# A graph network's edge stage and tile periods: new lags and beats, large accumulators for keys, values and down projections, sums transposed behind the gate

## The chip, the core and the metric

The kernel runs on one core of a Trainium2 chip. The metric is the device time of one execution in microseconds (us), the median of the runs. One execution was also recorded by the hardware profiler, and every duration below is of that one. The engines are TensorE (PE: matrix products; PEld is its weight load), VectorE (DVE), ScalarE (ACT), GpSimd (POOL) and SyncE (SP). SP, ACT and POOL also issue DMAs, each in the order of its own instructions.

## What is computed

Two layers of a graph network run over 625 nodes with 1024 features and 10000 edges, followed by a mixture of experts. The change lies in the first layer. Cut to it, the reference is:

```python
xn = _layernorm(x)
x = x + graph_attention(xn, edges) + linear_attention(xn)   # both read the same xn
x = x + ffn(_layernorm(x))          # gate, up and down, weights cut to -1, 0, 1
xn = _layernorm(x)                  # from here the second layer
...
def graph_attention(x, src, dst):
    x = rmsnorm(x) @ W_down
    xl, xr = x @ Wl, x @ Wr
    e = sum_over_64(leaky_relu(xl[src] + xr[dst]) * att)    # four heads for every edge
    alpha = softmax of e over the edges of one dst
    return segment_sum(alpha * xl[src], dst) @ W_up
```

## The kernel before

Nodes are taken in five tiles of 125 (t = 0 to 4), features in eight chunks of 128. Products are in float32, and one product of the source is two MATMUL instructions in the profile. The order of every engine's instructions is written out by hand (a manual schedule). A small queue `do` spreads a step over time: `do(prep, pe, after, after2)` writes the PE work now, `after` at the next call of `do`, and `after2` at the one behind that. So the place of a call in the code sets its place on each engine.

**Edge stage** (about 50 to 430 us). PE works on the linear attention: keys and values of all tiles (`key`, `value`) in two halves c = 0 and 1, counts of edges (`count`), queries and answers, then its output projection in pieces (`mixed`). Beside it, POOL, DVE and ACT work on the edges in *beats* of two columns of 128 edges. In a beat, POOL gathers rows of xl and xr (`gather`, lines 585 to 593), DVE adds and weighs those of an earlier beat (`score_group`), ACT takes the exponential (`raise_all`), and POOL scatters an older result into a table in DRAM (`scatter`). `lags = [3, 4, 5]` says how many beats behind the gather the score, the exponential and the scatter are. Four buffers hold gathered rows. PE's program calls `work(us)` behind each piece of its work, and a beat is written out when the sum of these passes a due time:

```python
while beat["us"] >= 8.0 + 5.2 * min(beat["g"], 5) + 8.1 * max(beat["g"] - 5, 0) and chunks:
```

Beats 1 to 5 also hold the self loops of one tile each. From the end of the queries on, the lags are 1, 1 and 2. `weight_sums` (line 741, DVE) and `weight_means` (a small product pm on PE) make the scales of the feed-forward weights, and `ternary` cuts them.

**The gate.** When the last scatter is in the table, `load_table(t)` fetches the exponentials of all edges into tile t, in `[src, dst]` order: two DMAs, 1.2 MB. `weigh(t)` on DVE multiplies them by the edge counts, and `sums(t)` on PE (pg) adds them up. Table 0 goes through ACT's queue, tables 1 to 4 and the five tiles of x (0.5 MB each) through POOL's.

**Tile periods** (p = 0 to 6, about 430 to 620 us). In period p, tile p gets its sums (pg), the division go, the transpose `turn_sums` (pgoT, copied by ACT to goT) and the product with W_up (`up_again`, px). Tile p - 1 gets the feed-forward network: statistics and quantisation on DVE (p1), transposes (f1, ptr), gate and up products (f2, pgu), a transpose (f3, phT), and the down product (f4, pdn). Tile p - 2 is normalised and transposed for the second layer (p5, f5). From period 2 on, keys and values of the second layer (pk, pv; `spacer`) fill in. Their weights are 4 MB, issued by SP (`lin1.weights(0)`).

PSUM has two pools of accumulators there: `ps1`, two of 512 columns, and `ps2`, three of twice 512. A new accumulator waits until an old one of its kind has been read. The output projection holds three large ones until `up_again` of tiles 0, 1 and 2 has added to them.

`class LinearAttention` (line 216) serves both layers: `half(c)` loads weights and two rows of biases, broadcast to 128 partitions.

Of the kernel before, what the change touches and what calls it, by code (L numbers as in the profile page):

```python
# [8 lines left out]
FP = mybir.dt.float32  # L9
# [44 lines left out]
def attempt(ctx: ExitStack, tc: tile.TileContext, w: dict, out: bass.AP, shifted: bool):  # L54
# [161 lines left out]
    class LinearAttention:  # L216


        def __init__(self, xnT, names, bq, work, rows_on):
            self.xnT, self.names, self.work, self.rows_on = xnT, names, work, rows_on  # L220
            self.bq = mix.tile([128, KC], FP, tag="bq", name="bq", bufs=2)
            rows_on.dma_start(out=self.bq, in_=bq)
            self.kv = []
# [8 lines left out]

        def half(self, c, loaded=False):
            Wk, bk, Wv, bv = (w[n] for n in self.names[1:])
            if not loaded:
                self.weights(c)
            self.bk, self.bv = self.bias(bk, c, "bk_t"), self.bias(bv, c, "bv_t")
            self.kf = mid([P, NT, 512], "kf")
            self.v = mid([P, NT, 4, 129], "v")
            nc.gpsimd.memset(self.v[:, :, :, 128:129], 1.0)  # L240
            self.kv.append(mix.tile([128, 4, 256], FP, tag="kv", name="kv", bufs=2))

        def key(self, t):
            kf, bk, wk = self.kf, self.bk, self.wk

            def pe():
                hold["pk", t] = ps1("pk")
                group(hold["pk", t][:P], [(self.xnT[:, k, nodes(t)], wk(k)) for k in range(KC)])

            def after():  # L250
                kb = mix.tile([P, 512], FP, tag="kb", name="kb", bufs=1)
                nc.vector.tensor_tensor(kb, hold.pop(("pk", t))[:P], bk[:P], op=ALU.add)
                ke = mix.tile([P, 512], FP, tag="ke", name="ke", bufs=1)
                nc.scalar.activation(ke, kb, AF.Exp)
                nc.scalar.activation(kb, kb, AF.Relu)
                hold["k", t] = ke, kb

            def after2():
                ke, kb = hold.pop(("k", t))
                nc.vector.scalar_tensor_tensor(kf[:, t, :], ke, 1.0, kb, op0=ALU.min, op1=ALU.add)  # L260

            do(None, pe, after, after2)
            self.work(7.0)

        def value(self, t):
            v, bv, wv = self.v, self.bv, self.wv

            def pe():
                hold["pv", t] = ps1("pv")
                group(hold["pv", t][:P], [(self.xnT[:, k, nodes(t)], wv(k)) for k in range(KC)])  # L270

            def after():
                nc.vector.tensor_tensor(v[:, t, :, 0:128],  # L273
                                        hold.pop(("pv", t))[:P].rearrange("p (a b) -> p a b", a=4),
                                        bv[:P].rearrange("p (a b) -> p a b", a=4), op=ALU.add)

            do(None, pe, after)
            self.work(7.0)
# [64 lines left out]
    with ExitStack() as st0:  # L343
# [8 lines left out]
        with ExitStack() as edges:  # L352
# [232 lines left out]
            def gather(g, j, side):  # L585
                lo, n, p = groups[g]
                if j == 0 and side == 0:
                    ab[g] = [pool.tile([128, G, 256], FP, tag=k, name=k, bufs=4) for k in ("ga", "gb")]
                if j < n:
                    src, ix = ((xl_d, si), (xr_d, di))[side]  # L590
                    nc.gpsimd.indirect_dma_start(  # L591
                        out=ab[g][side][0:p, j, :], out_offset=None, in_=src[:, :],
                        in_offset=bass.IndirectOffsetOnAxis(ap=ix[0:p, lo + j:lo + j + 1], axis=0))
# [9 lines left out]

            def scatter(last):

                if chunks and chunks[0][0] <= last:
                    g, j = chunks.pop(0)
                    lo, n, p = groups[g]
                    nc.gpsimd.indirect_dma_start(  # L609
                        out=table[:, :],  # L610
                        out_offset=bass.IndirectOffsetOnAxis(ap=at[0:p, lo + j:lo + j + 1], axis=0),
                        in_=es[0:p, lo + j, :], in_offset=None)
# [33 lines left out]


            beat = dict(us=0.0, g=0, scored=0, raised=0)
            lags = [3, 4, 5]

            def scores(last):
                while beat["scored"] <= min(last, len(groups) - 1):
# [1 line left out]
                    beat["scored"] += 1  # L654

            def raise_all(last):
                while beat["raised"] <= min(last, len(groups) - 1):
                    lo, n, p = groups[beat["raised"]]
                    exp(es[0:p, lo:lo + n, :])
                    beat["raised"] += 1  # L660

            def one_beat():
                g = beat["g"]
                beat["g"] += 1
                if 1 <= g <= NT:
                    self_loops(g - 1)
                if lags[1] > lags[0]:
                    raise_all(g - lags[1])
                    scores(g - lags[0])
                else:  # L670
                    scores(g - lags[0])
                    raise_all(g - lags[1])
                for j in range(G):
                    if g < len(groups):
                        gather(g, j, 0)
                        if lags[1] == lags[0]:
                            scatter(g - lags[2])
                        gather(g, j, 1)
                    scatter(g - lags[2])

            def work(us):
                beat["us"] += us

                while beat["us"] >= 8.0 + 5.2 * min(beat["g"], 5) + 8.1 * max(beat["g"] - 5, 0) and chunks:
                    one_beat()

            work(0.0)
# [27 lines left out]
                f()  # L715


            def mixed(t, ks=range(KC), keep=None):
                for c in range(2):
                    def pe(c=c):  # L720
                        if c == 0 and ks[0] == 0:
# [8 lines left out]
                            nc.vector.tensor_tensor(keep[:, c, :], px[:P, c, :], bo[c][:P], op=ALU.add)  # L730

                    do(None, pe, after if keep is not None and c == 1 else None)
                    work(0.87 * len(ks))

            dn = main.tile([128, 2, D], BF, name="dn")
            part3 = main.tile([128, 3], FP, name="part3")
            wmean = main.tile([128, 3], FP, name="wmean")
            wscale = main.tile([128, 3], FP, name="wscale")
# [23 lines left out]
                                        op0=ALU.subtract)  # L762

            for m in range(KC):
                if m + 1 < KC:
                    lin.query(m + 1)
                else:
                    mixed(0, range(6))
# [8 lines left out]
            wu = wpool.tile([128, 2, D], FP, tag="w", name="wu")  # L777
            nc.sync.dma_start(out=wu, in_=w["W_up"].rearrange("(k p) n -> p k n", p=128))
            bo = [lin.bias(w["L0_bo"], c, tag) for c, tag in enumerate(("bk_t", "bv_t"))]
            gu = wpool.tile([128, KC, 512], BF, tag="w", name="gu", padded_shape=[128, KC, 512])  # L780
            made = [gu[:, :, 0:256], gu[:, :, 256:512], dn]
            lags[:] = 1, 1, 2
            kept = mid([P, 2, 2, 512], "kept")
            mixed(3, keep=kept[:, 0])
            weight_sums()
            mixed(4, keep=kept[:, 1])
            weight_means()
            mixed(0, range(6, KC))
# [12 lines left out]
        late = st0.enter_context(tc.tile_pool(name="l0r", bufs=1, reuse_waits="tile"))  # L801


        def load_table(t, eng=nc.gpsimd):

            hold["tb", t] = mid([P, NT, P, 4], "tb")
            if not shifted:
                rows_dma(eng, hold["tb", t].rearrange("p s d h -> p s (d h)"),
                         tview[:, :, t * 4 * P:(t + 1) * 4 * P])

        def weigh(t):
# [105 lines left out]
        def ffn(t):  # L917
# [55 lines left out]

            def f4():
                def pe():
                    hold["pdn"] = [ps1("pdn") for c in range(2)]
                    for c in range(2):
                        group(hold["pdn"][c][:P], [(hT[:, k, 0:P], dn[:, k, c * 512:(c + 1) * 512])
                                                   for k in range(2)])

                def after():
                    rd = late.tile([P, 1], FP, tag="rd", name="rd", bufs=2)
                    nc.vector.tensor_scalar(rd, wmean[:P, 2:3], rh[:, t:t + 1], None, op0=ALU.mult)
                    for c in range(2):
                        xc = x[:, t, c * 512:(c + 1) * 512]
                        nc.vector.scalar_tensor_tensor(xc, hold["pdn"][c][:P], rd, xc, op0=ALU.mult, op1=ALU.add)  # L986

                do(None, pe, after)

# [16 lines left out]
            return p1, f1, f2, f3, f4, p5, f5  # L1006


        load_table(0, nc.scalar)
        for t in range(NT):  # L1010
            rows_dma(nc.gpsimd, x[:, t, :], xrows[t])
        load_table(1)
# [9 lines left out]
        for p in range(NT + 2):  # L1022
# [3 lines left out]
            if 1 <= p <= NT:  # L1026
                made_of[p - 1] = ffn(p - 1)
                made_of[p - 1][0]()
            if p >= 3:
                spacer()  # L1030
            if p >= 2:
                made_of[p - 2][6]()
            if p == 0:
                xnT1 = bigT("xnT1")
                nc.gpsimd.memset(xnT1[:, :, N:NP], 0.0)
                lin1 = LinearAttention(xnT1, ("L1_Wq", "L1_Wk", "L1_bk", "L1_Wv", "L1_bv"), w["L1_bq"],
                                       lambda us: None, nc.gpsimd)
            if p < NT:
                sums(p)
            if 1 <= p <= NT:  # L1040
                made_of[p - 1][1]()
                do()
                made_of[p - 1][2]()
            do()
            if p + 1 < NT:
                weigh(p + 1)
            if p + 2 < NT:
                load_table(p + 2)
            for t in ((0, 1), (2, 3, 4))[p] if p < 2 else ():
                for c in range(2):  # L1050
                    xc = x[:, t, c * 512:(c + 1) * 512]
                    nc.vector.tensor_tensor(xc, xc, bo[c][:P] if t < 3 else kept[:, t - 3, c, :], op=ALU.add)
            if p == 0:
                lin1.weights(0)
            if p == 1:
                lin1.half(0, loaded=True)
            if 2 <= p <= NT:
                spacer()
            if p < NT:
                turn_sums(p)  # L1060
            if 1 <= p <= NT:
                made_of[p - 1][3]()
            do()
# [867 lines left out]
```

## Time and profile before

| | |
|---|---|
| median of 3 runs | 2233.98 us |
| lowest, highest | 2232.08, 2243.11 us |
| the profiled execution | 2229.6 us |
| its span, first to last instruction | 2227.7 us |
| mean granted PE clock | 0.979 |
| PE busy | 2121.2 us, 95% of the span |
| POOL busy | 341.9 us, 15% |
| last scatter of the edge stage starts | 412.5 us |
| first sums of period 0 (pg) start | 433.4 us |

How to read the lines: a timeline has the start, the duration, the engine, the line of the kernel and the operation, output <- inputs with shapes, and in brackets how long the engine had been idle before and what released it. A list of waits has the engine and the tile it was about to write, what it waited for, the sum in us, the number of times and the longest. L130 is the line of a helper through which nearly all products go, so one goes by the names of tiles. A table of windows gives the busy time of each engine in a stretch, the granted clock as a part of full speed, and what the DMAs moved.

### The profile page before, as it was taken

To read this page: it belongs to the slowest core of one execution; us is meant where nothing else is said; L and a number is where in the kernel's file an instruction comes from. 1 tells how busy PE (TensorE), PEld (TensorE's weight loads), DVE (VectorE), ACT (ScalarE), POOL (GpSimd) and SP (SyncE) were. 2 spreads that over 40 slices of the span, in tenths; PEclk is the share of its full clock that TensorE was granted. 3 is DMA by queue.
4 is the path that set the end of the run, shared out by engine and by line. 5 is a ranking of instruction groups with operands and counts; after the bars stand their busy time and mean duration, and the time that the engine had idled before them with its cause. 6 is when DMAs were issued, how large, how long until landed. Compare 5 with 4: busy or idle time off the path is not lost. (4 is left out here: it accounts for less than half of the span.)

```text
span 2227.7 us, 17364 instructions
## 1 busy us (share of the span) xinstructions
PE 2121.2 (95%) x6934; PEld 1213.9 (54%) x6934; DVE 715.2 (32%) x1216; ACT 194.5 (9%) x354; POOL 341.9 (15%) x349
## 2 busy tenths in 40 slices
PE   7999898778899989999999999999999999999998
PEld 6665574444455667754445767557744444444443
DVE  4866395566521670000113133322010111111112
ACT  2100110011211110000000111110000000000000
POOL 1677777300000130010000000110000000000011
PEclk9999999869999999999999999999999999999999
DMA  9343342530122110231213111031199987997742
GB/s 289 116 136 109 119 139 86 153 92 0 38 85 76 48 48 0 76 142 38 76 38 104 38 38 38 20 103 55 41 346 337 331 325 282 327 330 287 275 144 92
DMA packets 146246, 301.62 MB, mean 135 GB/s; under 512 B 12361, under 2 KB 23052, under 8 KB 146152
## 3 DMA queue, kind: packets, MB, share of 16 engines
q1 hardware_dynamic: 123412, 243.18, 30.7%
q0 software_dynamic: 17408, 46.22, 6.8%
q10 hardware_dynamic: 5332, 10.97, 1.6%
q8 instruction: 58, 0.95, 0.2%
q14 instruction: 36, 0.29, 0.0%
HBM read 277.49 MB, written 22.84 MB: 135 GB/s over the span
## 5 line engine op out<-in xcount | busy, mean ns | idle before, releaser
L130 PE MATMUL pu<-w,xgT 128*128 128x512 f32 x768 | 333.9, 593 | 1.9 <-DVE xgT L1225 1.9
L130 PEld LDWEIGHTS pu<-w,xgT 128*128 128x128 f32 x768 | 144.0, 190 | 174.8 <-issue 171.7
L130 PE MATMUL pyb<-w,hb 128*128 128x512 f32 x384 | 174.3, 598 | 2.4 <-ACT yb L105 2.1
L130 PE MATMUL pq<-xnT,w 128*128 128x313 f32 x512 | 140.6, 434 | 9.4 <-DVE v L273 8.1
L130 PE MATMUL pv<-w,xnT 128*125 128x512 f32 x320 | 142.7, 599 | 4.7 <-DVE x L986 4.7
L130 PE MATMUL pk<-w,xnT 128*125 128x512 f32 x320 | 140.6, 592 | 0.0
L130 PE MATMUL p<-tT,w 128*128 128x313 f32 x512 | 136.3, 428 | 0.4 <-DVE tT L1225 0.4
L130 PEld LDWEIGHTS pq<-xnT,w 128*128 128x128 f32 x512 | 98.1, 193 | 50.5 <-DVE v L273 9.0
L130 PEld LDWEIGHTS pyb<-w,hb 128*128 128x128 f32 x384 | 69.8, 189 | 90.9 <-issue 74.8
L1765 DVE TENSOR_TENSOR su<-pu,su 128x512 f32<-128x512 f32 x24 | 16.6, 691 | 314.6 <-ACT su L1764 314.6
L130 PEld LDWEIGHTS p<-tT,w 128*128 128x128 f32 x512 | 96.8, 190 | 37.9 <-issue 1.2
L130 PEld LDWEIGHTS pv<-w,xnT 128*125 128x125 f32 x320 | 59.9, 190 | 79.1 <-issue 72.5
L130 PEld LDWEIGHTS pk<-w,xnT 128*125 128x125 f32 x320 | 59.6, 188 | 71.6 <-issue 71.0
L609 POOL DMA_INDIRECT table<-es,at x79 | 83.5, 1056 | 59.9 <-issue 28.9
L1748 POOL DMA_INDIRECT xg<-rows_d,slots x12 | 11.3, 943 | 524.8 <-PE pxg L1755 449.0
L591 POOL DMA_INDIRECT gb<-xr_d,di x79 | 83.5, 1057 | 24.1 <-issue 23.8
L591 POOL DMA_INDIRECT ga<-xl_d,si x79 | 79.7, 1009 | 32.1 <-issue 22.1
L724 PE MATMUL px<-w,oT 128*125 128x512 f32 x160 | 71.0, 605 | 0.8 <-DVE z L336 0.8
L130 PE MATMUL px<-w,hT 128*125 128x512 f32 x160 | 70.3, 592 | 0.0
L130 PE MATMUL px<-w,oT 128*125 128x512 f32 x160 | 70.3, 592 | 0.0
L1115 DVE TENSOR_TENSOR z<-pz,z 125x512 fp32r<-125x512 f32 x10 | 6.9, 692 | 196.8 <-ACT z L1113 196.8
L130 PE MATMUL ph<-meanT,w 128*128 128x313 f32 x256 | 70.1, 426 | 0.0
(368 smaller groups left out, 2534.4 us busy)
## 6 DMA issues: line engine op xcount, KB each, us to landing
w<-in_eW_dram SPq DMA_DIRECT2D x144, 1024.0 KB, 12.7
w<-in_L_Wk_dram SPq DMA_DIRECT2D x8, 1024.0 KB, 5.1
w<-in_L_Wv_dram SPq DMA_DIRECT2D x8, 1024.0 KB, 5.2
w<-in_L_Wq_dram SPq DMA_DIRECT2D x8, 1024.0 KB, 11.3
w<-in_L_Wo_dram SPq DMA_DIRECT2D x8, 1024.0 KB, 5.0
w<-in_W_self_dram SPq DMA_DIRECT2D x8, 1024.0 KB, 5.0
w<-in_W_neigh_dram SPq DMA_DIRECT2D x8, 1024.0 KB, 5.1
w<-in_sW_dram SPq DMA_DIRECT2D x8, 1024.0 KB, 6.4
```

Of the source, the lines that this page charges most:

```text
L130: nc.tensor.matmul(dst, lhsT=lhsT, rhs=rhs, start=(i == 0), stop=(i == len(pairs) - 1))
L591: nc.gpsimd.indirect_dma_start(out=ab[g][side][0:p, j, :], out_offset=None, in_=src[:, :], in_offset=bass.IndirectOffsetOnAxis(ap=ix[0:p, ...
L609: nc.gpsimd.indirect_dma_start(out=table[:, :], out_offset=bass.IndirectOffsetOnAxis(ap=at[0:p, lo + j:lo + j + 1], axis=0), in_=es[0:p, l ...
L724: nc.tensor.matmul(hold["px", t][:P, c, :], lhsT=oT[:, k, nodes(t)], rhs=wo[c](k), start=(k == 0), stop=(k == KC - 1 and keep is not None))
L1115: nc.vector.tensor_tensor(low, src, high.bitcast(FP), op=ALU.subtract)
L1748: nc.gpsimd.indirect_dma_start(out=xg, out_offset=None, in_=rows_d[:, :], in_offset=bass.IndirectOffsetOnAxis(ap=slots[:, b:b + 1], axis=0))
L1765: nc.vector.tensor_tensor(su, pu[:, 0, :], su, op=ALU.mult)
```

## The change

It has four parts.

- **Edge stage.** Five buffers for gathered rows instead of four; lags 4, 5, 6 instead of 3, 4, 5, cut by one at each of the last two of the eight queries; first beats due 6 us earlier, later ones every 8.5 us instead of 8.1; self loops in beats 5 to 9; a second scatter slot within a beat for scatters that are a beat behind; guards that let an exponential not pass its score and a scatter not pass its exponential. The sums of weights are taken within `mixed(3)`, ahead of its beats. The down projection's weights `dn` lie in another buffer.
- **Biases** are loaded ahead of the weights in `half`.
- **Table 0** goes through POOL's queue like the others. The weights of the second layer's keys and values are written in period 1 instead of 0.
- **Tile periods.** Keys, values and down projections use large accumulators, and `turn_sums` stands right behind the gate and up products, ahead of `weigh` and of the key.

```diff
 class LinearAttention:
+            self.large = False
         def half(self, c, loaded=False):
+            self.bk, self.bv = self.bias(bk, c, "bk_t"), self.bias(bv, c, "bv_t")
             if not loaded:
                 self.weights(c)
-            self.bk, self.bv = self.bias(bk, c, "bk_t"), self.bias(bv, c, "bv_t")
...
-                hold["pk", t] = ps1("pk")
+                hold["pk", t] = ps2("pk")[:, 0, :] if self.large else ps1("pk")
...
-                hold["pv", t] = ps1("pv")
+                hold["pv", t] = ps2("pv")[:, 0, :] if self.large else ps1("pv")
...
-                    ab[g] = [pool.tile([128, G, 256], FP, tag=k, name=k, bufs=4) for k in ("ga", "gb")]
+                    ab[g] = [pool.tile([128, G, 256], FP, tag=k, name=k, bufs=5) for k in ("ga", "gb")]
...
-                if chunks and chunks[0][0] <= last:
+                if chunks and chunks[0][0] <= min(last, beat["raised"] - 1):
...
-            lags = [3, 4, 5]
+            lags = [4, 5, 6]
...
-                while beat["raised"] <= min(last, len(groups) - 1):
+                while beat["raised"] <= min(last, beat["scored"] - 1):
...
-                if 1 <= g <= NT:
-                    self_loops(g - 1)
+                if 5 <= g < NT + 5:
+                    self_loops(g - 5)
...
                         gather(g, j, 0)
-                        if lags[1] == lags[0]:
-                            scatter(g - lags[2])
+                        scatter(g - lags[2] - 1)
                         gather(g, j, 1)
                     scatter(g - lags[2])
...
-                while beat["us"] >= 8.0 + 5.2 * min(beat["g"], 5) + 8.1 * max(beat["g"] - 5, 0) and chunks:
+                while beat["us"] >= 2.0 + 5.2 * min(beat["g"], 6) + 8.5 * max(beat["g"] - 6, 0) and chunks:
                     one_beat()
...
-            def mixed(t, ks=range(KC), keep=None):
+            def mixed(t, ks=range(KC), keep=None, then=None):
...
                     do(None, pe, after if keep is not None and c == 1 else None)
+                    if then is not None and c == 0:
+                        then()
                     work(0.87 * len(ks))
...
-            dn = main.tile([128, 2, D], BF, name="dn")
...
             for m in range(KC):
+                if m >= KC - 2:
+                    lags[:] = [n - 1 for n in lags]
...
+            dn = mix.tile([128, 2, D], BF, tag="kv", name="dn", bufs=2)
...
-            mixed(3, keep=kept[:, 0])
-            weight_sums()
+            mixed(3, keep=kept[:, 0], then=weight_sums)
...
-        def load_table(t, eng=nc.gpsimd):
+        def load_table(t):
...
-                rows_dma(eng, hold["tb", t].rearrange("p s d h -> p s (d h)"),
+                rows_dma(nc.gpsimd, hold["tb", t].rearrange("p s d h -> p s (d h)"),
...
-                    hold["pdn"] = [ps1("pdn") for c in range(2)]
+                    hold["pdn"] = ps2("pdn")
...
-        load_table(0, nc.scalar)
+        load_table(0)
...
+            if p == 1:
+                lin1.weights(0)
             if p >= 3:
                 spacer()
...
+                lin1.large = True
             if p < NT:
                 sums(p)
...
             do()
+            if p < NT:
+                turn_sums(p)
             if p + 1 < NT:
                 weigh(p + 1)
...
-            if p == 0:
-                lin1.weights(0)
             if p == 1:
                 lin1.half(0, loaded=True)
             if 2 <= p <= NT:
                 spacer()
-            if p < NT:
-                turn_sums(p)
```

More of the change, by code (lines that the diff above doesn't have):

```diff
@@ L975, in pe @@
                 def pe():
-                    hold["pdn"] = [ps1("pdn") for c in range(2)]
+                    hold["pdn"] = ps2("pdn")
                     for c in range(2):
-                        group(hold["pdn"][c][:P], [(hT[:, k, 0:P], dn[:, k, c * 512:(c + 1) * 512])
+                        group(hold["pdn"][:P, c, :], [(hT[:, k, 0:P], dn[:, k, c * 512:(c + 1) * 512])
                                                    for k in range(2)])
@@ L985, in after @@
                         xc = x[:, t, c * 512:(c + 1) * 512]
-                        nc.vector.scalar_tensor_tensor(xc, hold["pdn"][c][:P], rd, xc, op0=ALU.mult, op1=ALU.add)
+                        nc.vector.scalar_tensor_tensor(xc, hold["pdn"][:P, c, :], rd, xc, op0=ALU.mult, op1=ALU.add)
                 do(None, pe, after)
```

## The prediction

> **What bounds the kernel now.** I read the page first, then tables of windows, then the waits of each engine, then the timelines of the stretches that wait.
>
> The page: TensorE (PE) is busy in 95% of the span, so only its gaps and its slow stretches can be won. Its row of slices and the row of its granted clock show where: the eighth and ninth slice of 55.7 us, 390 to 501 us.
>
> ```profile
> span 2227.7 us, 17364 instructions
> PE 2121.2 (95%) x6934; PEld 1213.9 (54%) x6934; DVE 715.2 (32%) x1216; ACT 194.5 (9%) x354; POOL 341.9 (15%) x349
> ...
> PE   7999898778899989999999999999999999999998
> ...
> PEclk9999999869999999999999999999999999999999
> ```
>
> Windows over the edge stage up to its last scatter, over its second half, and over the tile periods (columns: window, length, busy PE, PEld, DVE, ACT, POOL, granted clock, DMA share, GB/s). In the tile periods PE idles 188.9 - 146.8 = 42.1 us, and the clock is 0.86.
>
> ```profile
> 56.00:413.00 357.00, 333.08 (x1215) 202.56 (x1214) 244.36 (x446) 34.99 (x94) 246.51 (x238) 0.97 0.34 110
> 229.70:429.70 200.00, 176.81 (x555) 103.41 (x553) 119.62 (x140) 17.18 (x42) 134.39 (x137) 0.94 0.37 114
> 429.70:618.60 188.90, 146.80 (x529) 85.94 (x529) 111.51 (x217) 30.99 (x48) 6.09 (x10) 0.86 0.22 63
> ```
>
> Waits of PE (total, times, longest): two in the edge stage (pm, pq), the others in the tile periods. VectorE (DVE) itself waits for gathers.
>
> ```profile
> PE pm L130 <- DVE part L743: 14.2, 1, 14.2
> PE pq L130 <- DVE v L273: 8.1, 1, 8.1
> PE pg L130 <- DVE pT L818: 5.1, 5, 3.6
> PE pv L130 <- DVE x L986: 4.7, 4, 1.4
> PE px L881 <- ACT goT L869: 4.0, 4, 1.2
> PE phT L967 <- DVE kb L252: 3.5, 3, 1.7
> ```
>
> ```profile
> DVE ga L599 <- DMA gb<-xr_d,di: 67.9, 16, 8.6
> DVE pT L818 <- DMA tb<-table: 20.0, 1, 20.0
> DVE kb L252 <- DMA bk_t<-in_L_bk_dram: 9.4, 1, 9.4
> ```
>
> GpSimd (POOL), timeline: its last scatter ends the edge stage; the first table load follows on ScalarE's (ACT) queue.
>
> ```profile
> 412.53 0.85 POOL L609 DMA_INDIRECT table<-es,at  x1 [1.91 <-issue]
> 414.49 0.33 ACTq L164 DMA_DIRECT2D tb<-table  x1
> 433.38 0.43 PE L130 MATMUL pg<-xl,pT 125*125 125x65 f32 x2 [3.64 <-DVE pT L818]
> 541.58 0.38 PE L865 MATMUL pgoT<-ident,go 125*128 125x125 f32 x2
> 543.65 0.43 PE L967 MATMUL phT<-ident,room 125*128 125x125 f32 x2 [1.69 <-DVE kb L252]
> 545.24 3.70 PE L881 MATMUL px<-wu,goT 128*125 128x512 f32 x8 [1.16 <-ACT goT L869]
> 551.23 7.13 PE L130 MATMUL pv<-w,xnT 128*125 128x512 f32 x16 [1.43 <-DVE x L986]
> ```
>
> The sums go against the profiled execution: 2229.6 us, of them 2227.7 span and 1.9 around it. The median of the runs is 2234.0; I move it by the same microseconds.
>
> **Part 1, edge stage: lags 4, 5, 6, five buffers, new beats, later self loops.** POOL issues 237 indirect DMAs, 246.7 us busy plus 0.30 between any two (71 us): 318 us from 56.1, so it could end at 374; it ends at 413.4. Of its waits, 9.1 (scatter for ACT's first exp) and 3.0 (gather for a buffer) lie before 98 us; five buffers and six beats before the first scatter remove these 12.1. Two more waits for ACT (2.4 at 276.8, 1.9 at 399.4) go with the longer lag: 4.3. At the end eight scatters stand back to back, from 391.3 to 412.5 at 3.0 us each, against 1.3 between gathers. By the order in the code the shortened lags and the extra scatter slots leave six: 2 x 1.7 = 3.4. The waits for scatters to land amid weight loads (4.2, 1.9, 3.8) stay. POOL ends at 413.4 - 12.1 - 4.3 - 3.4 = 393.6; bounds 374 and 413.
>
> DVE has POOL's gathers one beat (8 us) earlier in its order, longer than most of its waits for gb (3 to 5 us). So PE's 8.1 (v behind a score) and 14.2 (the sums of weights, 6.7 us, now ahead of two beats) go, and the half clock behind each: pq 11.26 instead of 8.59, and 1.6 in the px behind pm (72 at 27.73/64 would be 31.2, they took 32.8). PE's end of this stage moves from 429.7 by 26.6 to 403.1. If DVE waits again at the cut lags, down to nothing of the 26.6. The self loops (3.8 us of DVE each, ten small DMAs on ACT's queue) move from about 64 to 94 us to 77 to 112; DVE is then above 90% full, but it has gained the 9.4 below; PE's waits for the ring were 0.7 in all, bounds -0.7 to +3. The guards in exp and scatter add no instruction. dn now takes the buffer of the first half's state, last read by the fourth answer (po near 309), well before ternary writes it (406.8): nothing.
>
> **Biases ahead of weights in `half`.** First half: bk_t was issued at 48.9 behind Wv and held DVE 9.4 us with PE covered; now 0.5 MB goes ahead of Wk. SyncE's (SP) third and fourth weight DMAs waited 7.4 us for an xl_d write[...]. Two DMAs more in front can put Wk on that wait: issue near 45 instead of 39.4, landing 5.1 later, against PE at 47.9. Between 0 and 5 us; I take 2. Second half: the biases wait for c = 0's last key and value (143.7, 157.7), and now Wk, Wv, Wq and the raw weights queue behind them on SP. Wk was fetched at 50; now it is asked for at about 155 to 158, and PE wants it at 162.1, with 5.1 for landing: 0 to 4 us, I take 1.5. PE ends at 406.6.
>
> **Part 2, the gate: table 0 on POOL's queue, ahead of x.** It waits about 2 us for the last scatter, is issued near 396, and holds back ten loads of x (5.6 us of issue), table 1 and bq; x is first used after period 0. As it is, the load was issued at 414.5 beside 2.5 MB of x and landed 17.8 us later; on POOL's queue the four others took 7.0, 7.5, 9.6, and 15.2 among x and weights. [...] by the rows 7.0 to 15.2. I take 10, since SP's 4 MB of keys' and values' weights start near 396 too: pg at 407, just behind PE's 406.6, instead of 433.4.
>
> I see no effect in writing the weights' load one period later: on SP nothing lies between the two places, and its wait was for PE's px, released chunk by chunk. So the weights still share the DMAs, and **table 1** is late next. Tables, x and weights are 9 MB, moved from 414.5 to 448, with table 1 landed at 441.2 and not waited for. The same 26.7 us after 396 gives 423, all bytes first 429; I take 425. DVE waits in its order there for weigh(1) (4.85), with four x additions (2.4) and period 0's own addition behind it, then the chain to the next ptr (6.8, from 452.6 to 459.4): 425 + 1 + 4.85 + 2.4 + 6.8 = 440. It was 459.4, so **-19.5**. If the weights do move, table 1 lands by 415 and PE's own work sets about 431: -28. If it lands no earlier than before, -4. Period 1 itself keeps its waits: hT stands behind weigh(2) and the additions (3.5), xn (4.2), and the half clock.
>
> **Part 3, tile periods.** Keys, values and down projections leave the two small accumulators for the three large ones; pgoT comes before the key. In order then: pgu, pgoT, key, phT, px, pdn, value. Period 3: from the end of the key (541.6) to px at 545.24 were 3.6; phT alone is 0.43, and goT is copied under the key (-2.8). DVE's hT, at 545.97, just meets px's new end near 546. pdn ends at 549.8 and pv starts at 551.23: -1.4. Transposes behind pv no longer share with it: 0.7 + 0.3 = -1.0. Together -5.2. Period 2 by the same rows: -3.8 before px and pdn's end, -1.4: -5.2. Period 4: -1.7 - 1.4 - 1.0 = -4.1. Period 5 has no px; pdn waits 2.95 for hT behind kb and kf as before: -1.4. Period 6: -0.3. Sum **-16.2**. The new wait would be for the third large accumulator: a value needs the one released two allocations ago, at most an addition of 1.2 behind px. Bounds -6 (hT late by 2 a period) and -20.
>
> **Sum:** -19.5 - 16.2 = -35.7: 2193.9 profiled, 2198 beside the median. Behind 618.6 nothing changes; PE is full there.
>
> **Rivals.**
> - *Weights no longer collide, or the clock stays up in periods 0 and 1:* -28 - 16.2 = -44 to -52 with the half clock's 8: 2182 to 2190. For it: pg(0) took 10.8 at half clock and 4.5 at full. Against: nothing on SP holds the weights back.
> - *The gate does not move:* POOL still ends near 413 because landings of scatters, not lags, hold it (17.3 us of waits for table landings speak for it); only part 3 stays: 2218.
> - *Accumulators gain nothing:* hT, behind weigh and kb, becomes the bound: -20: 2214. Or the change does not do what it says at all, and each wait only changes its name: 2230.
> - *Slower:* the lags are cut at the seventh and eighth query. If POOL is then over two beats (16 us) late, DVE stands at beats 35 to 37 in front of the last answers, which PE needs: three waits as long as the longest now (8.6) are 26, with half clock behind them 39. Against it, 8.1 + 2.7 and 16.2 gained elsewhere, 27: +12, 2246. Against this rival: POOL's lateness by my count is about 13 us at beat 34.
>
> **How the numbers follow.** Sum as worked: 0.52, own range 2186 to 2210. Weights or clock better: 0.20. Gate fixed: 0.10. Accumulators nothing: 0.08. Nothing: 0.05. Slower: 0.05. What this kernel's measurement can tell from no change is about 0.5%, 11 us: faster is under 2223, slower over 2245. The first four give 0.88 faster (a little of them lands within), 0.08 within, 0.04 slower. The range leaves out the best of the second case, the worst of the third and the last two: 2176 to 2220.
>
> **What would show it.** Right: pm's and pq's waits gone, last scatter near 394, ptr of period 1 near 440 with DVE waiting for table 1, phT waiting no more for kb and px no more for goT, 28 to 29 us between pg(3) and pg(4) instead of 34. Wrong: SP issuing the weights only after pg(0); key waiting for Wk near 48 or 162 by over 5; DVE waits for gb at beats 35 to 37; pdn waiting for hT in each period.

## The result, and the profile after

The changed kernel takes 2214.86 us (median of 4 runs, 2212.67 to 2217.86) against 2233.03 for the kernel before, run beside it (median of 4 runs); the ratio is 0.9913 with a 95% interval of 0.9890 to 0.9936. That is 18.2 us faster, half of the 35.7 that were forecast, inside the range of 2176 to 2220 and 17 us off the number of 2198. The profiled execution took 2212.67 us with a span of 2210.6, 17.1 under the span before.

The page of the kernel after: PE is busy as long as before (2119.9 us against 2121.2), so over the whole span the gain is idle time. The weak slices are still there, now the seventh to the ninth of 55.3 us each.

```profile
PE 2119.9 (96%) x6934; PEld 1215.4 (55%) x6934; DVE 714.3 (32%) x1216; ACT 194.3 (9%) x354; POOL 342.3 (15%) x351
...
PE   7999997869899989999999999999999999999998
```

Two events cut the run into what the change touched first and what it touched last: the transposes (ptr) of period 1, which start at 459.41 before and 461.10 after, and the key behind the last transposes of the tile periods, at 618.61 and 601.63. Up to the first of them the kernel after is 1.7 us *later*. Windows between the two events, before and then after (columns: window, length, busy PE, PEld, DVE, ACT, POOL, granted clock, DMA share, GB/s):

```profile
459.41:618.61 159.20, 126.13 (x439) 70.28 (x439) 92.64 (x189) 29.03 (x45) 3.27 (x6) 0.89 0.11 32
```

```profile
461.10:601.63 140.53, 120.37 (x439) 69.21 (x439) 92.60 (x189) 28.77 (x46) 3.27 (x6) 0.89 0.12 37
```

The stretch is 18.7 us shorter with the same instructions on PE and DVE: 12.9 us less idle time of PE (20.2 against 33.1) and 5.8 us less busy time. So the tile periods brought the whole gain, and the edge stage, the gate and table 1, for which -19.5 was forecast, brought +1.7.

The timeline of PE in period 3 of the kernel after shows how: the transposes of h (phT) and the product px have no wait in brackets any more, the down projection waits 0.46, and the value follows at once. From pg(3) to pg(4) are 28.3 us (519.39 to 547.70), where there were 34.0.

```profile
534.37 0.38 PE L970 MATMUL phT<-ident,room 125*128 125x125 f32 x2
534.59 3.60 PE L884 MATMUL px<-wu,goT 128*125 128x512 f32 x8
538.64 1.08 PE L130 MATMUL pdn<-dn,room 128*125 128x512 bf16 x4 [0.46 <-DVE room L973]
```

In the waits of PE up to 660 us (total, times, longest) pm's 14.2 and pq's 8.1 are gone (0.0 and 0.8), but others stand in their place:

```profile
PE pg L130 <- DVE pT L821: 12.0, 10, 6.4
PE px L724 <- DVE z L337: 11.3, 1, 11.3
...
PE pk L130 <- DMA w<-in_L_Wk_dram: 3.2, 1, 3.2
```

The timeline of DVE shows where the 11.3 come from. The score at 355.31 stands in DVE's order ahead of z, the divisor of the last answer; its gather is late, z is late with it, and the output projection px of node tile 3 starts at 358.43 instead of 347.

```profile
355.31 0.69 DVE L600 TENSOR_TENSOR ga<-ga,gb 128x512 f32<-128x512 f32 x1 [6.93 <-DMA gb<-xr_d,di]
...
357.57 0.80 DVE L337 TENSOR_SCALAR z<-pd 128x626 f32<-128x626 f32 x1
```

The timeline of POOL, the last gather, the first and last of the six scatters behind it, and table 0. Before, the last scatter was issued at 412.53 and table 0 at 414.49: it hardly moved. The six scatters are (409.18 - 392.33) / 5 = 3.4 us apart, and table 0 waits another 4.7 for the last one to land.

```profile
391.17 0.86 POOL L592 DMA_INDIRECT gb<-xr_d,di  x1 [0.30 <-issue]
392.33 1.00 POOL L610 DMA_INDIRECT table<-es,at  x1 [0.30 <-DMA table<-es,at]
...
409.18 0.85 POOL L610 DMA_INDIRECT table<-es,at  x1 [2.75 <-issue]
414.73 0.89 POOL L164 DMA_DIRECT2D tb<-table  x1 [4.70 <-DMA table<-es,at]
```

Behind it the gate does come forward: table 0 lands in 8.7 us instead of 17.8, and pg(0) starts at 425.39 instead of 433.38. The 8 us are lost again one step on, where DVE waits for table 1. Before, weigh(1) started at 444.96 without a wait. Table 1 is issued later than before (430.90 against 425.99), since the loads of x in front of it on POOL's queue now stand behind table 0 and wait 3.7 us for it to land. The 4 MB of weights, on SP's queue, go out earlier (from 408.75 against 419.47), since PE's px lets go of their buffers earlier.

```profile
447.16 4.83 DVE L821 TENSOR_TENSOR pT<-tb,CT 125x500 f32<-125x500 f32 x5 [10.14 <-DMA tb<-table]
```

### The profile page after: what moved, and what is told of

Same layout as the page of the kernel before. It is cut to its first block, busy times and chain, and to the rows that moved or that the text cites. A ratio compares the mean times of both kernels' runs of the same rounds, so it can differ in the third digit from the quotient of the medians.

```text
span 2210.6 us, 17366 instructions
## 1 busy us (share of the span) xinstructions
PE 2119.9 (96%) x6934; PEld 1215.4 (55%) x6934; DVE 714.3 (32%) x1216; ACT 194.3 (9%) x354; POOL 342.3 (15%) x351
## 5 line engine op out<-in xcount | busy, mean ns | idle before, releaser
L592 POOL DMA_INDIRECT gb<-xr_d,di x79 | 78.9, 998 | 24.1 <-issue 23.5
L724 PE MATMUL px<-w,oT 128*125 128x512 f32 x160 | 71.1, 605 | 11.3 <-DVE z L337 11.3
```

Source lines behind the costliest of these rows:

```text
L592: nc.gpsimd.indirect_dma_start(out=ab[g][side][0:p, j, :], out_offset=None, in_=src[:, :], in_offset=bass.IndirectOffsetOnAxis(ap=ix[0:p, ...
L724: nc.tensor.matmul(hold["px", t][:P, c, :], lhsT=oT[:, k, nodes(t)], rhs=wo[c](k), start=(k == 0), stop=(k == KC - 1 and keep is not None))
```

## The experiments

Theory T, formed from these two traces: the tile periods give all of the gain. In the edge stage POOL's chain ends where it did, so whatever PE gains or loses there is hidden in front of the gate; and behind the gate table 1, which shares the DMA engines with x and 4 MB of weights (DMA share 1.05 and 256 GB/s from 425 to 445 us), ends later than the gate. Its rivals stand in each expectation. The numbers of the experiments name their runs further on.

**1 and 2: each half of the change alone.** The first takes the kernel before and adds the large accumulators and the moved `turn_sums`; the second takes the kernel after and takes these out. The cut shows the lines that the first adds.

```diff
-                hold["pk", t] = ps1("pk")
+                hold["pk", t] = ps2("pk")[:, 0, :] if self.large else ps1("pk")
...
-                    hold["pdn"] = [ps1("pdn") for c in range(2)]
+                    hold["pdn"] = ps2("pdn")
...
+            if p < NT:
+                turn_sums(p)
             if p + 1 < NT:
                 weigh(p + 1)
```

> The kernel before with the tile periods' edits alone: large accumulators for keys, values and down projections, the transposes of the gate's sums right behind the gate. Theory T (the whole gain comes from these periods, because POOL's chain in the edge stage ends where it did): 2214 to 2218, 16 to 19 us under the kernel before. Rival R (both halves of the change gain about the same, and the profiled executions mislead): 2223 to 2226. In the trace by T: ptr of period 1 at 459 to 460 as before, the end of the keys near 601, pm's wait of 14 and pq's of 8 still there.

> The kernel after without the tile periods' edits: edge stage, order of biases and weights, and table 0 on POOL's queue are new, the periods are the old ones. Theory T: 2231 to 2237, no different from the kernel before. Rival R: 2222 to 2226. In the trace by T: ptr of period 1 at 460 to 462, 34 us from pg(3) to pg(4).

The periods alone: 2215.18 us, ratio 0.9936 (0.9915 to 0.9957). Everything else alone: 2230.88 us, ratio 0.9992 (0.9981 to 1.0003). Both are T's (the second by 0.1 under its range); the rival's 2222 to 2226 is out for both. The two gains add up to 20.1, the whole change gave 18.2. In the trace of the first the two events stand at 459.48 and 602.60, and pm waits 13.4 and pq 8.5, as before. One forecast for the second missed: from pg(3) to pg(4) were 37.7 us and not 34, in its slowest execution (2236.16), which is the one in the trace. There pg(3) took 7.86 us against 4.58 in the kernel before, the median of all of pg's matmuls was 417 ns against 273, and the mean granted clock of the execution 0.974 against 0.979.

The pair, run on one chip, also shows the gate's gain being given back. With table 0 on ACT's queue (first) it is issued at 416.26, DVE's weigh(0) starts at 431.61 and pg(0) at 432.70; with table 0 on POOL's queue (second) it is issued at 415.85, weigh(0) starts at 425.37 and pg(0) at 426.46. But weigh(1) starts at 445.27 in the first and at 447.29, after a wait of 9.2, in the second, and period 1's ptr at 459.48 and 461.24.

**3: the lags are not cut.** The two lines that shorten them at the seventh and eighth query are taken out.

```diff
-                if m >= KC - 2:
-                    lags[:] = [n - 1 for n in lags]
```

> The kernel after with the lags left at 4, 5, 6 through the seventh and eighth query. Theory T (the cut puts scores 33 to 35 in front of answer 7's z, and that is the new wait of 11.3 us at the px of node tile 3; but POOL, not PE, sets the gate): the wait goes, PE ends its share of the edge stage near 408 instead of 419, then stands 15 us or more for pT, and the total is 2211 to 2216, 0 to 4 us under the kernel after. Rival A (the wait and the half clock behind it cost their full length): 2201 to 2205. Rival B (the cut was what kept the tail of scatters short): POOL's last scatter moves from 409 to 415 or later, and the total is 2219 to 2223.

2213.01 us (0.9911, 0.9895 to 0.9928). T, and half of rival B: px's wait is gone and PE ends its share of the stage at 373.52 + 31.14 = 404.7, 14 us earlier than the 419.0 (387.88 + 31.14) of the kernel after. But the scatters that the cut would have brought forward now stand at the end; the last is issued at 415.86, table 0 at 418.46, and PE stands in front of the gate. The wait changed its name and its place:

```profile
428.13 0.68 PE L130 MATMUL pg<-xl,pT 125*125 125x65 f32 x2 [23.47 <-DVE pT L819]
```

**4: the weights really later.** In the change, `lin1.weights(0)` is written a period later, but on SP's queue nothing holds it back: its four DMAs go out at 408.8, 412.2, 415.6 and 419.1, as the chunks of px let go of their buffers. Here they are issued on POOL's queue at the place where they are written, behind tables 0 to 2 and x. (The lines that hand the queue down to the DMA are left out.)

```diff
             if p == 1:
-                lin1.weights(0)
+                lin1.weights(0, nc.gpsimd)
```

> The kernel after with the four DMAs of the next attention's key and value weights (4 MB) issued on POOL's queue at the place where the program writes them, behind tables 0 to 2 and x, instead of on SP's queue. Theory T (table 1 is late because those weights share the DMA engines with it): table 1 lands in 7 to 9 us instead of 15, DVE's wait of 10.1 for it shrinks to 3 or less, and the total is 2203 to 2209, 6 to 12 us under the kernel after. Rival C (table 1 is bound by x in front of it and by its own rows): no change, 2213 to 2217. Rival D (the weights, issued near 450, now come after the first key asks for them near 482): a wait of up to 10 us there, 2215 to 2225.

2204.87 us, ratio 0.9876 (0.9857 to 0.9895): 8 to 10 us under runs 1 and 3, which ran on the same chip. Table 1, issued at 425.69, is there when DVE has waited 2.54 instead of 10.14, and period 1's ptr comes 10.5 us earlier than 461.10. The first key, at 490.78, does not wait.

```profile
436.63 4.90 DVE L821 TENSOR_TENSOR pT<-tb,CT 125x500 f32<-125x500 f32 x5 [2.54 <-DMA tb<-table]
```

**5 and 6: on top of the late weights**, the lags not cut, and table 1 issued ahead of x.

```diff
         load_table(0)
+        load_table(1)
         for t in range(NT):
             rows_dma(nc.gpsimd, x[:, t, :], xrows[t])
-        load_table(1)
```

> Both of the last two edits on the kernel after: lags left at 4, 5, 6 through the last queries, and the next attention's weights on POOL's queue. Theory T (POOL's tail of scatters sets the gate, and without the cut it is 3 to 5 us longer): PE's wait of 11 to 13 at the px of node tile 3 becomes one of 20 or more for pT; pg(0) starts near 425 to 428 instead of 422.5; total 2204 to 2209, no better than with the late weights alone (2204.9). Rival A (the two gains add): 2201 to 2203.

> The late weights, and table 1 issued right behind table 0, ahead of the ten loads of x. Theory T (behind the gate the path is DVE's: table 1's landing, weigh(1), the additions, the first norm): weigh(1) follows weigh(0) at once, ptr of period 1 comes 4 to 7 us earlier than 450.6, total 2198 to 2201. Rival C (x then lands later and DVE's additions wait for it, or pg(0) at half clock covers it): no gain, 2203 to 2207. Worse is possible if table 0 lands later for sharing with table 1: 2208.

Without the cut: 2205.58 us (0.9883, 0.9866 to 0.9899), no better than 4, as T says. px's wait of 12.7 in run 4 became one of 16.3 in front of pg(0), which starts at 421.37. I had expected 20 or more, and 425 to 428: POOL's last scatter was issued at 408.98, earlier than in run 3, so the longer tail of run 3 is not a rule. With table 1 first: ptr of period 1 at 446.99, 3.7 us earlier than in 4, but 2204.01 us (0.9881, 0.9859 to 0.9903), which is rival C's total and not T's. From there to the end of the periods it took 144.3 us against 141.6. PE's busy time makes nearly all of this, 124.9 against 122.4: the waits in periods 5 and 6 are the same, but the products behind them took longer (pgu of period 5 3.67 us against 2.48, the last value 8.33 against 7.03). No gain is shown.

**7: a ceiling.** On top of run 5, the last 8 of the 40 groups of edges are left out. This also takes their scores from DVE and ACT.

```diff
+            groups = groups[:32]
```

> A ceiling: the late weights, lags not cut, and the last 8 of the 40 groups of edges (15 of 79 columns) left out, so that they are not gathered, scored or scattered; the experts' blocks later may then differ in number, so stage times count, not the total. Theory T (POOL's chain sets the gate, PE and DVE have room): POOL's last scatter lies 50 us or more earlier, table 0 is there before PE ends its share, pg(0) starts at 405 to 408 instead of 422 to 428, and ptr of period 1 at 430 to 436 instead of 450.6. Rival (PE or DVE would end there anyway): pg(0) no earlier than 418.

POOL's last scatter is at 353.48, table 0 is loaded before PE needs it, and pg(0) and ptr follow PE's own work, 17 and 26 us earlier than in run 4 (422.45 and 450.64). So in every version above it is the work on the edges that sets the gate: POOL's gathers, which z waits for, and its scatters. A part of the 26 is pg(0) itself: it takes 4.48 us here and 10.8 there, where the granted clock was 0.50 from 428 to 436.

```profile
405.25 4.48 PE L130 MATMUL pg<-xl,pT 125*125 125x65 f32 x40
...
424.49 1.66 PE L940 MATMUL ptr<-ident,room 125*128 125x125 f32 x8 [3.15 <-DVE dens L853]
```

Its tail shows the pace of scatters alone: 13 of them from 317.22 to 353.48, 36.3 / 12 = 3.0 us each.

**8: the beats closer together.** One number in the placement of POOL's beats, on top of the late weights.

```diff
-                while beat["us"] >= 2.0 + 5.2 * min(beat["g"], 6) + 8.5 * max(beat["g"] - 6, 0) and chunks:
+                while beat["us"] >= 2.0 + 5.2 * min(beat["g"], 6) + 8.0 * max(beat["g"] - 6, 0) and chunks:
```

> The late weights, and the beats of the edge stage placed every 8.0 instead of 8.5 us of planned PE work, so that beat 35 stands 14.5 us of PE work earlier. Theory T (POOL is held by the landing of scatters, each of which waits for the one before, and by its own issue, not by the beats' place in the program): the last scatter stays within 3 us of 410, DVE waits more for gathers (35 us or more instead of 25), total 2203 to 2208. Rival P (the beats' place holds POOL): the last scatter is 8 us or more earlier, total 2195 to 2199.

2212.06 us (0.9912, 0.9896 to 0.9929), 6.5 to 8 us over runs 5 and 6 beside it: slower than either theory said. T's mechanism holds: the last gather is issued at 385.10 instead of 391.98, the last scatter at 408.96 instead of 410.49. What T missed is the price on the other side. DVE waits 40.2 us for gathers instead of 25.2, part of it in front of z, and now PE is the late one:

```profile
374.47 29.53 PE L724 MATMUL px<-w,oT 128*125 128x512 f32 x64 [19.20 <-DVE z L337]
```

This is the wait of 11.3 in the kernel after at a larger size, made by asking for the scores too early.

**9: two tables.** The chip of runs 9 to 12 stretches the edge stage of every program: the kernel before took 2276.4 us there, and each of the four profiles has engines idle in this stage without a cause that it shows. The kernel after was not run there. So these four are compared with each other, and no total of theirs with the runs above. Run 9 takes the kernel after and scatters every second column of scores to a second table that nobody reads.

```diff
-                        out=table[:, :],
+                        out=(table, table2)[j][:, :],
```

> The kernel after, with every second column of edge scores scattered to a second table that nobody reads, so that a scatter no longer writes where the one before it did; half of the edges are then missing from the gate and the experts' blocks may differ in number, so the edge stage's times count, not the total. Theory T (what keeps POOL's end at 409 to 412 is that each scatter waits for the landing of the one before): POOL's waits for table landings fall from 15 us to 5 or less, the last scatters stand 1.3 to 1.5 us apart instead of 2.9, and the last one is at 380 to 397. Rival P (issue and the waits for scores hold it): the last scatter stays at 404 or later.

Where the last scatter lies can't be compared with 409, so that half of the question stays open. The other half is answered: POOL's wait for landings of scores is gone altogether (15.4 us in the kernel after, 16 to 25 in runs 10 to 12), and from the end of the last gather to the end of the last of the six scatters behind it are 453.57 - 445.13 = 8.4 us; in run 10, which has one table, they are 457.80 - 440.11 = 17.7. Two consecutive ones of each, first with two tables, then with one:

```profile
447.02 0.97 POOL L611 DMA_INDIRECT table<-es,at  x1 [0.30 <-issue]
448.30 0.96 POOL L611 DMA_INDIRECT table<-es,at  x1 [0.30 <-issue]
```

```profile
445.71 1.90 POOL L610 DMA_INDIRECT table<-es,at  x1 [1.41 <-DMA table<-es,at]
449.49 1.83 POOL L610 DMA_INDIRECT table<-es,at  x1 [1.88 <-issue]
```

**10 to 12: biases behind weights, table 0 on ACT's queue, a filler in front of pg(0).** The first two undo one edit each in the kernel after; the third adds a filler to run 6.

```diff
-            self.bk, self.bv = self.bias(bk, c, "bk_t"), self.bias(bv, c, "bv_t")
             if not loaded:
                 self.weights(c)
+            self.bk, self.bv = self.bias(bk, c, "bk_t"), self.bias(bv, c, "bv_t")
```

```diff
-        load_table(0)
+        load_table(0, nc.scalar)
```

```diff
+        def warm():
+            group(ps1("pw")[:P], [(oT[:, k % KC, nodes(2)], wo[1](k % KC)) for k in range(14)])
+
+        do(None, warm)
```

> The kernel after with the biases of keys and values behind their weights again, as before. Theory T (their new place costs PE some 3 to 6 us at the first key, and POOL's end hides it): the first key's wait for Wk of 3.2 and its half clock go, PE is 4 to 6 us earlier in the first half and waits that much more later on, total 2212 to 2217, as with them in front. Rival: the total gains what PE gains, 2208 to 2211.

> The kernel after with table 0 issued on ScalarE's queue again. Theory T (POOL's queue lands it in 9 us instead of 18, because it is then ahead of x, but the gate's 8 us are given back at table 1): pg(0) starts near 432 instead of 425, table 1 is asked for no later than now, ptr of period 1 at 461 to 464, total 2213 to 2218. Rival (the gate's 8 us are a real part of the gain): 2221 to 2224.

> Late weights, table 1 ahead of x, and 14 matmuls of 512 columns on data at hand (6 us, their result is not used) in front of pg(0). Theory H (pg(0) takes 10.8 us, as it runs at half clock behind PE's pause for table 0; without the pause it takes 4.5, as in the run with beats of 8.0): pg(0) starts at 424 to 425 and ends 2 to 3 us earlier than without the filler, px(0) runs at full clock, ptr of period 1 comes 3 to 5 us earlier than 447.0, total 2199 to 2202. Rival (the small matmuls of pg lower the clock themselves, or DVE's pieces of table 0 pace them): pg(0) ends no earlier, total 2204 to 2208.

Beside 2276.4 for the kernel before: 2264.45 (0.9959, 0.9932 to 0.9987), 2261.88 (0.9942, 0.9922 to 0.9962) and 2268.38 us (0.9973, 0.9955 to 0.9991). On the totals all three are inconclusive, since the kernel after has none on this chip. Of the traces this stands: with the biases behind, the first key starts at 46.14 without a wait and takes 7.03 us; with them in front it starts at 50.26 and 49.86, after waits of 1.6 and 1.3, and takes 7.1 (runs 11 and 12). In the kernel after, on its chip, it waited 3.2 and took 10.1, with a granted clock of 0.50 up to 54. Table 0 on ACT's queue was issued at 462.62 and used from 477.62, 15.0 later; on POOL's queue (run 10) at 459.56 and 469.43, 9.9 later. The filler could show nothing, since on this chip PE came to the gate later than table 0 anyway; pg(0) took 4.48 us.

## Where the prediction was right and where it failed

- **Part 3, tile periods: right, with some luck in the size.** -16.2 forecast, all of it waits of PE. Measured are -18.7 between the two events, -16.1 in the trace of run 1 and -17.9 in its medians. Waits are 12.9 of the 18.7 (12.2 in run 1). The rest is shorter busy time, in part because the half clock lasted less: px of period 2 took 5.34 us before and 3.60 after, at a mean granted clock of 0.69 and 1.00, the last value 8.81 and 7.62, at 0.81 and 0.92. The signs came as named: phT and px without waits, 28.3 us a period. Accumulators as the next bound did not show; pdn waits 0.5 for hT in period 3.
- **Part 1, POOL's end: failed, and with it half of the sum.** The step is "POOL ends at 413.4 - 12.1 - 4.3 - 3.4 = 393.6"; it ended at 410.0. The 12.1 were won at first, and the 3.4 at the end: the tail has six scatters, as counted, and took 18.0 us instead of 22.4. What failed is that nothing was put in the place of the waits taken away. Counted by POOL's indirect DMAs, the 25th starts 15.2 us earlier than before (2.6 of it because the first does), the 49th 6.3, the 85th 3.8 and the last 3.3.
  - *The first loss, between 88 and 122 us:* scatters now wait 3.5, 1.4, 2.9 and 1.5. By the profile the 1.4 and the 1.5 are for the landing of the self loops' writes, the 2.9 is for ACT, and the 3.5 has no cause shown. The prediction priced the later self loops for DVE and PE only, although each also issues two DMAs into the table to which the scatters go. The kernel before and run 1 have no such wait for self loops; runs 2 to 6 and 8, with the new edge stage, have 3.3 to 7.7 us of them.
  - *The second, between 161 and 184 us:* four waits, 11.1 us in all (the first, of 4.2, by the profile for ACT, the others for landing), where two of 4.2 and 1.9 stood that were to stay (in runs 2 to 6 and 8: four, 9.7 to 11.9 us). They stand beside SP's weight loads, which the new place of the biases has drawn together (DMA share 0.79 from 175 to 190 us, 0.21 before). That this is their cause was not tested.
  - *Of the 4.3,* only 0.6 went: ACT is waited for 1.8 at 280.9 and 1.9 at 395.3. The latter was misread. In the tail of the kernel before, every second scatter waits 1.9, whatever is named for it.
  - DVE's ternary ran from 396.3 to 407.6, and three scatters of the tail beside it took 1.4 to 2.3 us, as before.

From the kernel after, the wait for self loops (total, times, longest) and three of the second loss:

```profile
POOL table L610 <- DMA table<-own: 2.9, 2, 1.5
...
172.26 0.98 POOL L610 DMA_INDIRECT table<-es,at  x1 [2.75 <-DMA table<-es,at]
178.38 1.39 POOL L610 DMA_INDIRECT table<-es,at  x1 [2.23 <-DMA table<-es,at]
184.22 1.05 POOL L610 DMA_INDIRECT table<-es,at  x1 [1.93 <-DMA table<-es,at]
```

- **Why POOL's end answers so little: partly shown.** Where scatters follow each other into one table, POOL waits for landings: 3.0 us a scatter where no gathers lie between (run 7), against 1.3 to 1.6 and no such wait with two tables (run 9). Earlier beats only lengthen this tail (run 8: last gather 6.9 us earlier, last scatter 1.5). On the chips without the stretched edge stage no full run has its last scatter outside 408 to 416, whether the last gather was issued at 381 or at 392. How far POOL's end would come forward without the two losses above was not measured.
- **Part 1, PE's end: 403 to 407 forecast, 419.0 measured, 404.7 without the cut of the lags (run 3).** pq's and pm's waits went as forecast. The new wait of 11.3 in front of px is the one that the prediction described as its slower rival, "DVE stands in front of the last answers", at one wait instead of three. It cost nothing that the totals show (run 3), since POOL was later still.
- **Biases: about right, and hidden.** 3.5 forecast for wait and half clock at the first keys of the two halves; 6.6 in the kernel after, 0.6 to 5.1 in runs 2 to 4. Run 2, which has them, is no slower than the kernel before.
- **Part 2, table 0: right by the rows.** I took 10 from landings of 7.0 to 15.2 us on POOL's queue, and it was 8.7. From issue to use the tables 0 on ACT's queue took 15.0 to 17.8 us (before, runs 1 and 11), those on POOL's 8.3 to 9.9 (the kernel after, runs 2 to 6 and 10). On POOL's queue x stands behind the table and waits for it (3.7 us in the kernel after).
- **Table 1: the mechanism right, the place wrong.** It was named as late next, at 425; it landed at 447, because its issue hung on POOL's end and on x's wait for table 0. The size given for weights that do move, 8.5 us more (28 against 19.5), is what run 4 found: some 10.

The likeliest case lost to the rival "the gate does not move", 2218, which named the waits for landings as its evidence. The total alone could not have told: the measured 2214.86 is also the 2214 of the rival in which the accumulators gain nothing, and here they gained all of it. The prediction had the 3 us between scatters beside 1.3 between gathers, and used it for the tail alone. It did not ask for what other landings a scatter would have to wait from its new place.

## What to carry to other kernels

A wait that is removed counts only up to the next one on the same engine: list what the step's new place makes late, every DMA that it issues included. A transfer moved in the text of a program is not moved on a queue that nothing holds (written a period later, the weights here still went out from 408.75, even earlier than the 419.47 before); put it behind something on the same queue, as in run 4, the version that beats both kernels here. And where one chain sets a join, first leave a piece of that chain out and look at the ceiling before tuning the other side.

## What was not expected of the hardware

- Indirect scatters into one table started 3.0 us apart in this program (run 7), against 1.3 to 1.6 for scatters into two tables in turn (run 9). In ten of run 7's twelve steps the profile shows POOL waiting for an earlier scatter's DMA, 1.4 to 5.0 us each; in run 9 it shows no such wait. Whether the chip needs that wait was not tested.
- In run 4 PE paused for 2.2 us in front of pg(0) and for 0.5 us three times between its first pieces. The granted clock was 1.00 up to 424 us, 0.62 from 424 to 428, 0.50 to 436, 0.67 to 440 and 1.00 from 440 to 448, though PE was busy for 13.4 of the 16 us from 424 to 440. pg(0) took 10.8 us; without any pause it took 4.5 (runs 7 and 8). The last 7.0 us of pg(0), from 426.24, ran without a pause, and from 428 to 436 the clock stayed at 0.50. Nor do the pauses alone decide: behind pg(0), with the same two of 0.9 and 0.5 us, px took 3.70 us in run 8, where the clock stayed at 1.00, and 5.39 us in run 7. What else decides was not tested.
